# Moving a row of scores through memory in place of TensorE transposes, in a two-layer graph kernel

## The chip, the cores and the metric

The kernel runs on one core of a Trainium2 chip. The metric is device time in microseconds (us) of one execution, lower is better. In the profile of the kernel before, TensorE runs 14264 matrix products and transposes, VectorE and ScalarE run 3909 and 4811 operations, most of them on tiles of 128 partitions, GpSimd does 323 odd jobs, and SyncE is seen only issuing DMAs (transfers). They run side by side (of a span of 2377.1 us TensorE is busy for 2355.3, VectorE for 1988.5), each in the order that the program gives it: with one fetch moved ahead in SyncE's order, a wait of 207.5 us for it goes (e3). For each wait the profile names what ended it. Times are compared with runs of the kernel before taken on the same chip in the same rounds. All repeated runs here were in the normal, fast state; the five single looks (e9 to e11) are of unknown state, so their times are not argued from.

## The reference

128 graphs of 128 tokens with 512 features pass through two layers, all in float32. Layer 0 is multi-head attention weighted by the adjacency matrix. Layer 1 is graph attention:

```python
Wh = jnp.einsum('bsi,io->bso', hidden_state, W)
Wh1 = Wh @ a[:OUT_F, :]
Wh2 = Wh @ a[OUT_F:, :]
e = Wh1 + jnp.swapaxes(Wh2, 1, 2)
e = jax.nn.leaky_relu(e, negative_slope=ALPHA)
attention = jnp.where(adjacent_matrix > 0.5, e, NEG_INF)
attention = jax.nn.softmax(attention, axis=1)
h_prime = jnp.einsum('bst,bto->bso', attention, Wh)
return jax.nn.elu(h_prime)
```

Each token has two scalar scores. The matrix `e` needs one of them along the rows and the other along the columns. In the kernel a token is a partition, so one score is at hand as a number per partition, while the other has to reach all partitions as a row of 128 numbers. How that row gets there is the subject.

## The kernel before

The kernel works on pairs of graphs, 64 in all. A hand-written list (`ORDER`) says in which order the steps of pairs at different stages are issued, for example `pb:2` for "scores of the pair two behind". Each engine keeps to that order. The steps that matter, cut:

```python
def dot1(p, i, k):            # the two scores of each token, on VectorE
    h2, ws = h1s[p]
    ...
        junk, h2[:, i, :], 1.0, (us_sb, ut_sb)[k], ..., accum_out=ws[:, i, k : k + 1]

def scores1(p):               # step "pb": one score to all partitions, on TensorE
    ws = h1s[p][1]
    pb = ps1.tile([P, 2, S], F32, name="pb", tag="ps1")
    for i in range(2):
        nc.tensor.transpose(pb[:, i, :], ws[:, i, 0:1].to_broadcast([P, P]), ident)
    pbs[p] = pb

def mask1(p):                 # step "wm", on VectorE
    wts[p] = work.tile([P, 2, S], F32, name="w", bufs=2)
    nc.vector.scalar_tensor_tensor(wts[p], adjTs.pop(p), 0.5, pbs.pop(p), op0=OP.is_le, op1=OP.subtract)
```

Five transfers matter as well, four of them issued by SyncE. `blocks` and `aT` are a round trip that turns attention weights: 512 KB are written to memory after a transpose on VectorE, and read back in another arrangement. `hA` are the hidden rows of a later pair. `rows` and `mr` are another round trip: GpSimd writes two statistics per token to memory, and SyncE fetches them as one row for all partitions. `hidden` on VectorE then needs `mr`.

```python
def spread0(p):
    ...
    rows0[p] = dram.tile([2, P, 2], F32, name="rows0")
    nc.gpsimd.dma_start(rows0[p].rearrange("b p s -> p b s"), mv)

def fetch0(p):                # step "f0"
    ...
    nc.sync.dma_start(..., r.rearrange("b p s -> (b p s)").partition_broadcast(P))
```

## Time and profile before

| | before |
|---|---|
| median of 4 runs | 2380.38 us |
| span of the profiled run | 2377.1 us |
| TensorE busy / idle | 2355.3 / 21.8 us |
| VectorE busy | 1988.5 us |
| one cycle of two pairs in the middle | 73.08 us |
| granted TensorE clock | 1.000 |

The profile page gives each engine's busy time; "chain that ended last" follows the last instruction back through whatever released it. In its lines PE is TensorE (PEld its weight loads), DVE VectorE, ACT ScalarE, POOL GpSimd and SPq the queue of SyncE; L421 is line 421 of the kernel. The prediction below shows those lines. Two more belong to what follows. They list DMAs with their number, their size and the median time from issue to landing:

```profile
blocks<-tr SPq DMA_DIRECT2D x128, 512.0 KB, 5.1
...
rows<-mv POOLq DMA_DIRECT2D x60, 2.0 KB, 4.6
```

The second is a warning that is easily overlooked: 2 KB take nearly as long (4.6 us) as 512 KB (5.1 us).

### The profile page before, as it was taken

To read this page: it belongs to the slowest core of one execution; us is meant where nothing else is said; L and a number is where in the kernel's file an instruction comes from. 1 tells how busy PE (TensorE), PEld (TensorE's weight loads), DVE (VectorE), ACT (ScalarE), POOL (GpSimd) and SP (SyncE) were. 2 spreads that over 40 slices of the span, in tenths; PEclk is the share of its full clock that TensorE was granted. 3 is DMA by queue.
4 is the path that set the end of the run, shared out by engine and by line. 5 is a ranking of instruction groups with operands and counts; after the bars stand their busy time and mean duration, and the time that the engine had idled before them with its cause. 6 is when DMAs were issued, how large, how long until landed. Compare 5 with 4: busy or idle time off the path is not lost.

```text
span 2377.1 us, 40536 instructions
## 1 busy us (share of the span) xinstructions
PE 2355.3 (99%) x14264; PEld 2062.0 (87%) x14264; DVE 1988.5 (84%) x3909; ACT 1457.4 (61%) x4811; POOL 265.7 (11%) x323
## 2 busy tenths in 40 slices
...
GB/s 173 123 129 116 138 130 121 137 133 129 142 111 126 154 121 138 111 118 158 116 138 133 118 137 137 128 145 107 125 160 116 138 111 123 153 120 125 108 113 93
DMA packets 255275, 306.10 MB, mean 129 GB/s; under 512 B 21856, under 2 KB 181600, under 8 KB 254432
## 3 DMA queue, kind: packets, MB, share of 16 engines
...
HBM read 202.64 MB, written 100.79 MB: 128 GB/s over the span
## 4 chain that ended last, share of the span: by engine, by line
PE 99%; DMA 1%; DVE 0%; ACT 0%; issue 0%; DVEq 0%
PE acc_a L250 28%; PE row_a L291 24%; PE acc_c L250 14%; PE row_c L291 9%; PE acc_b L250 7%; PE sc L312 6%; PE pc L375 5%; PE pg L453 5%; PE pb L421 1%; DMA wk<-in_wkT 0%; PE pm L494 0%; DMA bq<-in_bq 0%; PE pt L189 0%; DVE junk L412 0%; DVE x L479 0%
## 5 line engine op out<-in xcount | busy, mean ns | idle before, releaser
L330 ACT ACTIVATE at<-at,nmx 128x128 f32<-128x128 f32 x1024 | 397.0, 393 | 23.0 <-DVE nmx L325 22.0
L291 PE MATMUL row_a<-w,gT 128*128 128x256 f32 x1280 | 325.4, 385 | 2.8 <-DVE z L471 1.7
L339 ACT ACTIVATE at<-at,rs 128x128 f32<-128x128 f32 x1024 | 317.8, 390 | 15.3 <-DVE rs L334 15.2
L291 PE MATMUL row_a<-wo,cxT 128*128 128x256 f32 x1280 | 319.5, 380 | 0.4 <-DVE cxT L148 0.4
L164 POOL TENSOR_SCALAR mv<-mv 128x2 f32<-128x2 f32 x128 | 78.9, 616 | 2057.8 <-DVE mv L161 1999.3
L467 ACT COPY z<-row_a 128x256 f32<-128x256 f32 x256 | 92.6, 362 | 298.5 <-PE row_a L291 297.9
L291 PEld LDWEIGHTS row_a<-w,gT 128*128 128x128 f32 x1280 | 237.3, 190 | 42.0 <-DVE z L471 2.5
L291 PEld LDWEIGHTS row_a<-wo,cxT 128*128 128x128 f32 x1280 | 233.8, 190 | 28.1 <-DVE cxT L148 0.6
L318 DVE SCALAR_TENSOR_TENSOR at<-sc,adj 128x1024 f32<-128x1024 f32 x128 | 156.7, 1225 | 92.2 <-PE sc L312 89.7
L267 ACT ACTIVATE kT<-acc_a,bk 128x256 f32<-128x256 f32 x256 | 107.3, 470 | 156.7 <-PE acc_a L250 155.1
L330 ACT ACTIVATION_READ_ACCUMULATOR at<-at,nmx 128x1 f32 x1024 | 195.5, 191 | 0.0
L346 DVE STREAM_TRANSPOSE tr<-at 128x1024 f32<-128x1024 f32 x128 | 158.7, 1240 | 33.0 <-ACT at L339 29.8
L160 DVE BATCH_NORM_STATS2 st<-x 128x6 f32<-128x512 f32 x256 | 175.3, 685 | 10.9 <-DMA x<-in_x 6.7
L389 DVE TENSOR_TENSOR x<-row_a,x 128x256 f32<-128x256 f32 x320 | 132.8, 415 | 50.6 <-PE row_a L291 48.3
L262 ACT COPY v<-acc_a 128x512 f32<-128x512 f32 x128 | 74.7, 584 | 150.0 <-PE acc_a L250 150.0
L325 DVE TENSOR_REDUCE nmx<-at 128x8 f32<-128x1024 f32 x128 | 156.1, 1220 | 4.2
L382 ACT COPY cxT<-pc 128x512 f32<-128x512 f32 x128 | 74.9, 585 | 127.3 <-PE pc L375 127.1
L312 PEld LDWEIGHTS sc<-kT,qT 64*128 64x128 f32 x2048 | 124.2, 187 | 32.4 <-issue 32.0
L312 PE MATMUL sc<-kT,qT 64*128 64x128 f32 x2048 | 148.7, 285 | 0.0
L165 POOL TENSOR_TENSOR mv<-mv,mhalf 128x2 f32<-128x2 f32 x128 | 140.2, 1095 | 10.7
L453 PEld LDWEIGHTS pg<-w,h 128*128 128x128 f32 x1024 | 133.7, 192 | 6.6 <-ACT z L467 0.2
L453 PE MATMUL pg<-w,h 128*128 128x128 f32 x1024 | 134.4, 275 | 0.0
...
## 6 DMA issues: line engine op xcount, KB each, us to landing
blocks<-tr SPq DMA_DIRECT2D x128, 512.0 KB, 5.1
aT<-blocks SPq DMA_DIRECT2D x512, 128.0 KB, 3.0
x<-in_x SPq DMA_DIRECT2D x123, 512.0 KB, 5.4
out<-x SPq DMA_DIRECT2D x64, 512.0 KB, 5.5
...
```

The source lines that it names most:

```text
L160: nc.vector.bn_stats(st, src[:, i, :])
L165: nc.gpsimd.tensor_tensor(mv[:, :, 1], mv[:, :, 1], mhalf.to_broadcast([P, 2]), OP.pow)
L250: nc.tensor.matmul(acc[:, m, :], lhsT, rhs, start=fresh and m == 0 and c == 0, stop=c == 1, skip_group_check=True)
L291: nc.tensor.matmul(acc, left[:, la, c, :], w[:, wb, c, :], start=n in (0, 3) and c == 0, stop=c == 1, skip_group_check=True)
L312: nc.tensor.matmul(sc[:, s * C + j, :], qT[r, j, cols], kT[r, j, cols], start=True, stop=True)
L318: nc.vector.scalar_tensor_tensor(at, scs.pop(b), QSCALE, adjs[p][:, i : i + 1, :].to_broadcast([P, H, S]), op0=OP.mult, op1=OP.mult)
L325: nc.vector.tensor_reduce(nmx, at, AX.X, OP.max, negate=True)
L330: nc.scalar.activation(at[:, j, :], at[:, j, :], AF.Exp, bias=nmx[:, j : j + 1], accum_out=sums[:, j : j + 1])
L339: nc.scalar.activation(at[:, j, :], at[:, j, :], AF.Copy, scale=rs[:, j : j + 1])
L346: nc.vector.transpose(trs[b], at.rearrange("p h (j k) -> p j h k", k=Q))
L389: nc.vector.tensor_tensor(d, row_acc(p, "o", bank), d, OP.add)
L453: nc.tensor.matmul(pg[:, c, :], h1s[p][0][:, i, c * P : (c + 1) * P], wts[p][:, i, :], start=True, stop=True)
```

## The change

TensorE is the bound, so take the 128 small transposes away from it, except in the last two pairs, where little other work would hide a round trip. In their place GpSimd writes the scores to memory, and SyncE reads them back into all partitions, straight into the tile that the mask operation then overwrites. The orders for the head, the loop and the tail were chosen anew.

```diff
+    def send_scores1(p):                                  # step "pd"
+        pbs[p] = dram.tile([2, P], F32, name="row1")
+        with nc.allow_non_contiguous_dma(reason="a number of a row"):
+            nc.gpsimd.dma_start(pbs[p].rearrange("b p -> p b"), h1s[p][1][:, :, 0])
+
+    def spread_scores1(p):                                # step "pv"
+        r = pbs[p]
+        pbs[p] = wts[p] = work.tile([P, 2, S], F32, name="w", bufs=2)
+        nc.sync.dma_start(
+            wts[p].rearrange("p b s -> p (b s)"), r.rearrange("b p -> (b p)").partition_broadcast(P)
+        )
 ...
+        if p < N - 2:
+            table.pop("pb")
+            table |= {"pd": lambda: send_scores1(p), "pv": lambda: spread_scores1(p)}
 ... (HEAD, ORDER and TAIL replaced; the part of the new ORDER that matters:)
+    d00:2 peb:1 d01:2 pd:2 ... fla:0 ... bla:0 w1:3 pv:2 ... lT:0 ... pla:0 ... f0:0 ... wm:2
```

On SyncE the new loop order reads: block send (`bla`), spread (`pv`), hidden rows (`lT`), block fetch (`pla`), statistics (`f0`).

More of the change, by code (lines that the diff above doesn't have):

```diff
@@ L422, in scores1 @@
         pbs[p] = pb
+    def send_scores1(p):
[8 more added lines that the diff above has]
+        )
     def mask1(p):
-        wts[p] = work.tile([P, 2, S], F32, name="w", bufs=2)
+        if p not in wts:
+            wts[p] = work.tile([P, 2, S], F32, name="w", bufs=2)
         nc.vector.scalar_tensor_tensor(wts[p], adjTs.pop(p), 0.5, pbs.pop(p), op0=OP.is_le, op1=OP.subtract)
@@ L535 @@
     HEAD = """
-        lx@0 t0@-5 Lu0@0 t1@-5 lt@0 Lq@0 Lk@0 pp@0 lx@1 hn0@0 hn1@0 tp0@0 Wq0@0 Lu1@0 t1@-4 t0@-4 tp1@0 pp@1 Wq2@0 hn0@1
-        ev0@0 Lv@0 ev1@0 U3@-1 U5@-1 Wk0@0 U1@-2 lx@2 hn1@1 F1@-2 tp1@1 Lo@0 tp0@1 Wq1@0 la@-1 Lw@0 ev0@1 la@0 ev1@1
-        t1@-3 t0@-3 U8@-2 U6@-2 F3@-1 pp@2 l0@-2 U2@-2 hs0@-3 F6@-2 l0@-1 hs1@-3 Wk1@0 U10@-2 Wv0@0 Lc@0 Wk2@0 Wk3@0
-        hn0@2 hs2@-3 U7@-1 F7@-1 Wv1@0 A5@-1 hs3@-3 t0@-2 U3@-2 F10@-2 t1@-2 pp@3 A8@-2 hn1@3 tp0@2 U2@-1 U9@-1 hn0@3
-        hn1@2 F3@-2 cu01@0 F2@-1 U4@-1 F9@-1 tp1@2 cu00@0 U8@-1 l0@0 ev0@2 ev1@2 A9@-1 U10@-1 tp0@3 Ww0@0 l0@1 t0@-1
@@ L541 @@
-        U11@-1 U5@-2 F4@-1 t1@-1 F10@-1 sca@0 F5@-2 tp1@3 ata@0 mxa@0 exa2@0 exa3@0 exa0@0 ccp@0 A2@-2 Wv2@0 ccd@0 U1@0
-        ev0@3 t1@0 sh@0 ev1@3 rca1@0 U6@0 U7@-2 nma2@0 Wq3@0 t0@0 F6@0 hs0@-1 cu10@0 s0@-1 nma3@0 exa1@0 U1@-1 rca0@0
-        lt@1 scb@0 hs1@-1 F7@-2 U3@1 nma0@0 nma1@0 A2@-1 fla@0 atb@0 U10@0 mxb@0 U6@-1 exb0@0 Wv3@0 U4@-2 t1@1 bla@0
-        U2@0 exb2@0 A11@-1 exb1@0 rcb0@0 exb3@0 t0@1 nmb0@0 A5@-2 f0@0 rcb1@0 nmb1@0 nmb3@0 pla@0 s0@0 A6@-1 Wo0@0 U9@-2
-        sup0@0 hs2@-1 nmb2@0 sca@1 Wo2@0 f0@1 flb@0 sua0@0 ata@1 blb@0 A9@-2 lT@1 F10@0 U8@0 F3@1 U2@1 A8@0 F1@0 mxa@1
@@ L546 @@
-        plb@0 la@1 cu11@0 hs3@-1 exa2@1 exa0@1 U3@0 F2@1 exa1@1 rca0@1 exa3@1 nma1@1 U5@1 U4@1 U7@1 A2@0 nma0@1 Wo1@0
-        Ww2@0 rca1@1 scb@1 F4@1 Ww1@0 nma3@1 nma2@1 lT@0 F7@1 l0@2 pca@0 F3@0 A5@1 fla@1 pcb@0 pea@0 sup1@0 U9@1 atb@1
-        mxb@1 peb@0 exb2@1 U8@1 U5@0 sua1@0 cs0@0 bla@1 s0@1 Ww3@0 hd0@0 pla@1 hd1@0 exb1@1 o0@0 f0@2 o1@0 F9@1 hd0@1
-        hd1@1 exb3@1 exb0@1 U10@1 od0@0 F10@1 cs1@0 od1@0 rcb1@1 nmb3@1 U1@1 rcb0@1 nmb2@1 F5@0 o2@0 nmb1@1 A9@1 sca@2
-        hs0@1 nmb0@1 A2@1 pca@1 U6@1 od2@0 Wo3@0 cs2@0 o4@0 flb@1 o3@0 ata@2 cs3@0 od4@0 U11@1 od4c@0 blb@1 o5@0 mxa@2
@@ L551 @@
-        o6@0 exa3@2 exa2@2 od5@0 hs2@1 exa0@2 exa1@2 U4@0 t1@2 rca1@2 nma3@2 hs1@1 A5@0 A6@1 od6@0 rca0@2 nma2@2 st0@0
-        U7@0 pea@1 nma0@2 U1@2 A11@1 st1@0 o0@1 plb@1 nma1@2 F7@0 pcb@1 scb@2 sh@1 fla@2 pw@0 peb@1 atb@2 U2@2 o1@1
-        mxb@2 F1@2 bla@2 nm@0 U3@2 h21@0 exb2@2 cs0@1 cs1@1 U4@2 U9@0 h20@0 A2@2 d11@0 od0@1 exb3@2 d00@0 od1@1 hs3@1
-        d10@0 F3@2 o2@1 lT@2 d01@0 od2@1 exb0@2 rcb1@2 pb@0 exb1@2 U5@2 wm@0 rcb0@2 pr@0 F5@2 nmb1@2 cs2@1 U6@2 m1@0
-        o4@1 e1@0 t0@2 lt@2 U7@2 nmb0@2 cs3@1 nmb3@2 A5@2 A9@0 pla@2 sw@0 F7@2 od4@1 o3@1 g0@0 nmb2@2 o5@1 ge0@0 od4c@1
+        lx@0 Lu1@0 Lo@0 Lw@0 t0@-5 lx@1 Lk@0 t1@-5 Lq@0 pp@0 hn0@0 hn1@0 tp0@0 ccp@0 ev0@0 t0@-4 lx@2 Lv@0 t1@-4 Lc@0
@@ new lines @@
+        pp@1 Wk0@0 Lu0@0 Wk2@0 hn0@1 tp1@0 hn1@1 tp0@1 cu10@0 ev1@0 tp1@1 ev0@1 U6@-2 Ww0@0 t0@-3 U3@-1 F6@-2 Ww1@0
+        ev1@1 t1@-3 U5@-1 F3@-1 Wk1@0 l0@-2 pp@2 Wq0@0 la@-1 Wo0@0 U8@-2 Wv0@0 Wq1@0 hs0@-3 U1@-2 hs1@-3 Wk3@0 ccd@0
+        U10@-2 F1@-2 Wv2@0 t0@-2 U7@-1 F10@-2 A5@-1 hn1@2 hn0@2 U2@-1 hs2@-3 F7@-1 t1@-2 Wq2@0 pp@3 U9@-1 F2@-1 hs3@-3
+        A8@-2 hn1@3 tp0@2 F9@-1 Wq3@0 U8@-1 ev0@2 hn0@3 Wv1@0 l0@-1 U4@-1 A9@-1 cu00@0 U10@-1 F4@-1 tp1@2 F10@-1 U3@-2
+        t1@-1 ev1@2 t0@-1 sca@0 F3@-2 l0@0 s0@-1 lt@0 U4@-2 ata@0 mxa@0 tp0@3 tp1@3 ev0@3 cu11@0 U1@0 exa2@0 ev1@3
@@ new lines @@
+        cu01@0 exa3@0 U11@-1 exa1@0 t0@0 exa0@0 f0@0 U5@-2 t1@0 A11@-1 s0@0 rca1@0 rca0@0 hs0@-1 U6@0 F5@-2 hs2@-1
+        nma2@0 sh@1 nma0@0 U2@-2 nma3@0 A5@-2 F1@0 Wv3@0 nma1@0 scb@0 F6@0 fla@0 U1@-1 U9@-2 A2@-1 atb@0 U6@-1 mxb@0
+        A9@-2 exb0@0 U7@-2 Ww3@0 exb1@0 hs1@-1 exb2@0 A6@-1 U3@1 lT@0 rcb0@0 exb3@0 lT@1 nmb0@0 rcb1@0 Wo1@0 U10@0
+        nmb1@0 A2@-2 l0@1 F7@-2 la@0 hs3@-1 nmb2@0 bla@0 sup0@0 nmb3@0 f0@1 sca@1 F3@1 flb@0 F10@0 U3@0 Wo2@0 blb@0 U2@1
+        ata@1 la@1 pla@0 U8@0 F2@1 mxa@1 F3@0 hd0@1 U5@1 exa0@1 plb@0 exa1@1 exa3@1 U7@1 rca0@1 t1@1 nma0@1 sh@0 exa2@1
@@ new lines @@
+        U5@0 nma1@1 A8@0 sua0@0 rca1@1 hd0@0 U4@1 F5@0 t0@1 nma2@1 nma3@1 s0@1 l0@2 scb@1 pca@0 F7@1 pcb@0 pea@0 fla@1
+        U9@1 peb@0 A5@1 bla@1 atb@1 o0@0 F9@1 mxb@1 o1@0 F4@1 exb1@1 U4@0 od0@0 Wo3@0 exb0@1 pla@1 cs0@0 exb3@1 rcb0@1
+        U7@0 cs1@0 hd1@1 nmb0@1 la@2 nmb1@1 od1@0 sup1@0 exb2@1 U10@1 sua1@0 rcb1@1 cs2@0 nmb2@1 hd1@0 U2@0 F10@1 nmb3@1
+        flb@1 o2@0 sca@2 Ww2@0 blb@1 od2@0 o3@0 A2@0 cs3@0 o4@0 A5@0 U9@0 od4@0 ata@2 plb@1 U1@1 od4c@0 mxa@2 o5@0
+        exa2@2 exa1@2 o6@0 od5@0 hs0@1 exa0@2 U1@2 rca0@2 od6@0 nma0@2 st1@0 exa3@2 pca@1 st0@0 scb@2 pea@1 rca1@2 hs1@1
@@ new lines @@
+        pw@0 nma3@2 A2@1 pcb@1 nma1@2 hs2@1 F7@0 U8@1 nma2@2 nm@0 peb@1 fla@2 h20@0 U6@1 h21@0 d00@0 F1@2 A9@1 d10@0
+        o0@1 atb@2 pd@0 U3@2 cs2@1 la@3 cs0@1 mxb@2 o1@1 F3@2 U11@1 cs1@1 exb0@2 od0@1 exb1@2 U5@2 A11@1 od1@1 hs3@1
+        U6@2 A9@0 pv@0 d01@0 bla@2 lT@2 rcb0@2 d11@0 nmb1@2 o2@1 f0@2 F5@2 U4@2 exb2@2 od2@1 exb3@2 F6@2 U7@2 pla@2 A5@2
+        A6@1 rcb1@2 wm@0 nmb2@2 o3@1 cs3@1 F7@2 o4@1 nmb0@2 pr@0 U2@2 od4@1 nmb3@2 od4c@1 m1@0 flb@2 e1@0 o5@1 o6@1
+        blb@2 od5@1 U9@2 od6@1 hd0@2 U10@2 st0@1 st1@1 plb@2 A2@2 pw@1 sw@0 hd1@2
@@ L556 @@
     """
     ORDER = """
-        F4:1 F6:1 flb:1 fb:4 U9:1 F9:1 g1:3 od5:2 ge1:3 o6:2 la:1 st0:2 s0:1 hd0:1 od6:2 U8:1 w0:3 st1:2 gs0:3 blb:1
-        hd1:1 pw:2 w1:3 gs1:3 nm:2 U10:1 zc0:3 so:4 U1:0 gs2:3 h20:2 A9:1 A8:1 l0:0 wd1:3 w2:3 F10:1 gs3:3 h21:2 plb:1
-        lx:1 hs0:1 zc2:3 lT:0 sca:0 pca:1 pcb:1 scb:0 w4:3 d00:2 d01:2 pea:1 A6:1 ata:0 mxa:0 peb:1 d10:2 w3:3 F1:0
-        d11:2 cs0:1 t1:0 exa1:0 f0:0 exa3:0 pb:2 sh:1 A4:4 wm:2 zc4:3 exa2:0 exa0:0 pr:2 o0:1 o1:1 rca1:0 F8:0 nma3:0
@@ L562 @@
-        hs2:1 w5:3 hs1:1 wd4c:3 rca0:0 U2:0 nma1:0 cs2:1 cs1:1 nma2:0 m1:2 nma0:0 w6:3 od0:1 U11:1 od1:1 fla:0 U3:0
-        zc5:3 atb:0 F2:0 mxb:0 F3:0 o2:1 e1:2 A10:16 cs3:1 wd6:3 U5:0 F5:0 sw:2 exb0:0 A2:0 U4:0 exb2:0 A3:28 exb3:0
-        exb1:0 A5:0 A11:1 bla:0 o3:1 rcb1:0 od2:1 nmb2:0 U6:0 hs3:1 o4:1 lt:0 rcb0:0 nmb0:0 t0:0 nmb3:0 nmb1:0 pla:0
-        U7:0 ez:3 F7:0 F11:-22 g0:2 fa:3 od4:1 A1:15 od4c:1 ge0:2 o5:1 A7:14
+        U1:0 F10:1 hs2:1 fb:4 t0:1 g0:3 so:4 g1:3 ge0:3 U2:0 t1:1 ge1:3 lt:2 nm:2 s0:1 F2:0 sca:0 h21:2 h20:2 pca:1
@@ new lines @@
+        ata:0 pcb:1 lx:1 pea:1 mxa:0 l0:0 A7:8 F1:0 scb:0 hs0:1 exa3:0 gs0:3 U4:0 hs1:1 exa2:0 hs3:1 gs2:3 d10:2 exa0:0
+        A2:0 U3:0 exa1:0 rca1:0 d00:2 peb:1 d01:2 pd:2 nma2:0 U8:1 F8:8 nma3:0 cs2:1 cs0:1 F11:-7 rca0:0 A4:8 A3:8 A1:8
+        cs1:1 nma1:0 A9:1 o0:1 nma0:0 gs1:3 o1:1 F4:0 fla:0 F3:0 w0:3 atb:0 bla:0 w1:3 pv:2 U5:0 mxb:0 F5:0 sh:1 zc0:3
+        lT:0 exb3:0 U11:1 od0:1 exb2:0 U6:0 od1:1 A5:0 exb1:0 pla:0 wd1:3 exb0:0 d11:2 o2:1 rcb1:0 A8:1 nmb3:0 U7:0 f0:0
+        od2:1 nmb2:0 A11:1 rcb0:0 cs3:1 nmb1:0 gs3:3 w2:3 wm:2 nmb0:0 F7:0 o4:1 F6:0 o3:1 zc2:3 od4:1 pr:2 flb:0 w3:3
@@ L566 @@
+        U9:0 od4c:1 blb:0 m1:2 F9:0 hd0:0 w4:3 A6:0 o5:1 zc4:3 e1:2 wd4c:3 o6:1 od5:1 plb:0 st0:1 A10:3 w5:3 sw:2 w6:3
+        od6:1 zc5:3 st1:1 la:-1 U10:0 wd6:3 pw:1 hd1:0 ez:3 fa:3
     """
     TAIL = """
-        F4@-5 U9@-5 F9@-5 g1@-7 flb@-5 o6@-6 A6@-5 U10@-5 fb@-8 la@-5 ge1@-7 gs0@-7 F10@-5 so@-8 hd0@-5 od5@-6 blb@-5
-        pca@-5 sca@-4 hd1@-5 pea@-5 la@-4 U5@-3 st0@-6 lx@-5 U8@-5 ata@-4 mxa@-4 exa0@-4 exa3@-4 exa1@-4 od6@-6 w0@-7
-        hs0@-5 w1@-7 o0@-5 scb@-4 exa2@-4 st1@-6 pw@-6 U3@-3 gs2@-7 A9@-5 zc0@-7 nm@-6 rca0@-4 rca1@-4 hs1@-5 wd1@-7
@@ L571 @@
-        nma3@-4 nma0@-4 gs1@-7 nma2@-4 o1@-5 gs3@-7 plb@-5 sh@-5 nma1@-4 fla@-4 pcb@-5 atb@-4 U11@-5 od0@-5 U6@-4 F3@-3
-        h21@-6 peb@-5 h20@-6 mxb@-4 exb0@-4 w2@-7 d10@-6 cs0@-5 exb3@-4 exb2@-4 zc2@-7 U7@-3 cs1@-5 A11@-5 d00@-6
-        exb1@-4 od1@-5 w4@-7 F6@-4 d11@-6 o2@-5 pb@-6 rcb0@-4 od2@-5 rcb1@-4 wm@-6 nmb1@-4 d01@-6 nmb0@-4 sca@-3 w3@-7
-        nmb2@-4 U10@-4 nmb3@-4 zc4@-7 w5@-7 cs2@-5 bla@-4 scb@-3 pr@-6 flb@-4 ata@-3 cs3@-5 hs2@-5 zc5@-7 pla@-4 m1@-6
-        wd4c@-7 pca@-4 mxa@-3 w6@-7 F7@-3 o4@-5 od4@-5 wd6@-7 F10@-4 e1@-6 U2@-3 blb@-4 exa1@-3 exa0@-3 sw@-6 plb@-4
@@ L576 @@
-        fa@-7 exa2@-3 o5@-5 ez@-7 pea@-4 rca0@-3 g1@-6 nma0@-3 exa3@-3 o3@-5 la@-3 od5@-5 U9@-3 st0@-5 rca1@-3 od4c@-5
-        g0@-6 o6@-5 ge1@-6 fb@-7 gs0@-6 o0@-4 A5@-3 nma2@-3 nma3@-3 pcb@-4 ge0@-6 nma1@-3 gs1@-6 w0@-6 o1@-4 fla@-3
-        atb@-3 so@-7 lx@-4 mxb@-3 F9@-3 od6@-5 w1@-6 F2@-3 peb@-4 hs3@-5 cs0@-4 zc0@-6 wd1@-6 st1@-5 U8@-4 U10@-3 pw@-5
-        bla@-3 exb3@-3 exb2@-3 exb1@-3 w2@-6 gs2@-6 gs3@-6 pla@-3 nm@-5 cs1@-4 exb0@-3 cs2@-4 rcb1@-3 la@-2 h21@-5
-        rcb0@-3 zc2@-6 nmb3@-3 A8@-4 U8@-3 nmb2@-3 sh@-4 nmb0@-3 nmb1@-3 F10@-3 w4@-6 od0@-4 d11@-5 cs3@-4 od1@-4 zc4@-6
@@ L581 @@
-        d10@-5 U4@-3 F4@-3 U1@-3 sca@-2 flb@-3 w3@-6 h20@-5 ata@-2 o3@-4 mxa@-2 w5@-6 wd4c@-6 zc5@-6 d00@-5 exa0@-2
-        o2@-4 od2@-4 w6@-6 o4@-4 A2@-3 d01@-5 wd6@-6 exa3@-2 od4@-4 lt@-4 exa1@-2 fa@-6 exa2@-2 pca@-3 ez@-6 U6@-3 pb@-5
-        fb@-6 rca0@-2 blb@-3 o5@-4 od4c@-4 wm@-5 nma0@-2 rca1@-2 pr@-5 od5@-4 nma3@-2 A6@-3 o6@-4 plb@-3 nma1@-2 U1@-4
-        U2@-4 nma2@-2 pcb@-3 m1@-5 scb@-2 st0@-4 pea@-3 od6@-4 st1@-4 fla@-2 e1@-5 A9@-3 so@-6 sw@-5 peb@-3 o0@-3 g1@-5
-        g0@-5 U11@-3 ge1@-5 pw@-4 atb@-2 lx@-3 o1@-3 F1@-4 ge0@-5 cs0@-3 nm@-4 mxb@-2 cs2@-3 h21@-4 exb1@-2 gs0@-5 o3@-3
@@ L586 @@
-        w0@-5 sh@-3 lt@-3 w1@-5 exb0@-2 exb3@-2 h20@-4 gs1@-5 od0@-3 A11@-3 U3@-4 exb2@-2 A2@-4 rcb0@-2 d10@-4 cs1@-3
-        zc0@-5 nmb0@-2 od1@-3 d00@-4 rcb1@-2 cs3@-3 o2@-3 d01@-4 wd1@-5 nmb1@-2 od2@-3 nmb2@-2 nmb3@-2 gs2@-5 sca@-1
-        pb@-4 gs3@-5 w2@-5 o4@-3 zc2@-5 w3@-5 flb@-2 od4@-3 ata@-1 d11@-4 wm@-4 w4@-5 zc4@-5 F3@-4 od4c@-3 o5@-3 pr@-4
-        w5@-5 zc5@-5 U5@-4 wd4c@-5 m1@-4 w6@-5 e1@-4 F5@-4 mxa@-1 o6@-3 od5@-3 st0@-3 sw@-4 exa2@-1 U4@-4 exa1@-1 od6@-3
-        exa0@-1 bla@-2 st1@-3 exa3@-1 g0@-4 pw@-3 g1@-4 wd6@-5 A5@-4 fa@-5 ez@-5 U9@-4 ge1@-4 nm@-3 rca0@-1 h21@-3 fb@-5
@@ L591 @@
-        blb@-2 h20@-3 ge0@-4 U7@-4 w0@-4 rca1@-1 gs0@-4 w1@-4 nma1@-1 nma2@-1 d10@-3 F7@-4 pla@-2 d00@-3 A9@-4 zc0@-4
-        gs1@-4 pb@-3 plb@-2 pca@-2 gs2@-4 d01@-3 d11@-3 nma3@-1 scb@-1 wm@-3 pcb@-2 wd1@-4 nma0@-1 peb@-2 w2@-4 so@-5
-        w3@-4 pr@-3 fla@-1 zc2@-4 w4@-4 atb@-1 lx@-2 pea@-2 mxb@-1 cs0@-2 exb2@-1 m1@-3 gs3@-4 zc4@-4 o0@-2 cs2@-2
-        wd4c@-4 cs1@-2 e1@-3 exb3@-1 o1@-2 sh@-2 exb1@-1 sw@-3 rcb1@-1 od0@-2 w6@-4 bla@-1 exb0@-1 w5@-4 zc5@-4 g1@-3
-        wd6@-4 od1@-2 ez@-4 rcb0@-1 nmb0@-1 o2@-2 nmb3@-1 pla@-1 fa@-4 lt@-2 fb@-4 o3@-2 nmb1@-1 g0@-3 nmb2@-1 ge0@-3
@@ L596 @@
-        ge1@-3 od2@-2 o4@-2 cs3@-2 w0@-3 flb@-1 od4@-2 gs0@-3 gs1@-3 o5@-2 od4c@-2 gs2@-3 o6@-2 so@-4 pca@-1 blb@-1
-        w1@-3 w3@-3 lx@-1 od5@-2 pea@-1 st0@-2 o0@-1 od6@-2 zc0@-3 o1@-1 st1@-2 gs3@-3 pw@-2 wd1@-3 nm@-2 h21@-2 w2@-3
-        sh@-1 od0@-1 od1@-1 h20@-2 zc2@-3 d10@-2 plb@-1 pcb@-1 peb@-1 d01@-2 w4@-3 d00@-2 cs0@-1 pb@-2 cs1@-1 wm@-2
-        d11@-2 o2@-1 zc4@-3 pr@-2 od2@-1 cs2@-1 m1@-2 w5@-3 cs3@-1 o4@-1 od4@-1 zc5@-3 o3@-1 o5@-1 wd4c@-3 e1@-2 od4c@-1
-        sw@-2 o6@-1 w6@-3 od5@-1 st0@-1 g0@-2 od6@-1 st1@-1 g1@-2 lt@-1 wd6@-3 ge0@-2 w0@-2 fa@-3 pw@-1 ge1@-2 gs2@-2
@@ L601 @@
-        w1@-2 ez@-3 nm@-1 gs0@-2 gs1@-2 h21@-1 zc0@-2 d10@-1 wd1@-2 h20@-1 d00@-1 d11@-1 d01@-1 w2@-2 pb@-1 zc2@-2 wm@-1
-        pr@-1 gs3@-2 w4@-2 zc4@-2 m1@-1 w3@-2 wd4c@-2 e1@-1 sw@-1 w5@-2 w6@-2 g0@-1 wd6@-2 g1@-1 zc5@-2 ge0@-1 ge1@-1
-        fb@-3 fa@-2 w0@-1 w1@-1 ez@-2 gs0@-1 gs2@-1 zc0@-1 gs1@-1 w3@-1 gs3@-1 wd1@-1 w2@-1 zc2@-1 w4@-1 fb@-2 zc4@-1
-        wd4c@-1 w5@-1 so@-3 so@-2 w6@-1 zc5@-1 wd6@-1 ez@-1 fa@-1 fb@-1 so@-1
+        g1@-7 g0@-7 ge1@-7 hs2@-5 F10@-5 U3@-3 fb@-8 nm@-6 so@-8 h21@-6 sca@-4 ge0@-7 pca@-5 ata@-4 pcb@-5 mxa@-4 scb@-4
@@ new lines @@
+        lx@-5 hs0@-5 exa3@-4 lt@-6 U8@-5 gs0@-7 exa2@-4 gs1@-7 h20@-6 U6@-4 exa1@-4 A9@-5 rca1@-4 exa0@-4 hs1@-5 d10@-6
+        nma2@-4 w0@-7 F6@-4 rca0@-4 d01@-6 U11@-5 pea@-5 d00@-6 nma0@-4 hs3@-5 pd@-6 nma3@-4 w1@-7 nma1@-4 peb@-5 U10@-4
+        fla@-4 zc0@-7 gs2@-7 wd1@-7 o0@-5 F10@-4 atb@-4 o1@-5 mxb@-4 w3@-7 pv@-6 bla@-4 U2@-3 A11@-5 exb1@-4 sh@-5
+        exb2@-4 w2@-7 exb0@-4 cs0@-5 cs1@-5 od0@-5 U8@-4 zc2@-7 od1@-5 exb3@-4 gs3@-7 rcb0@-4 pla@-4 rcb1@-4 w4@-7 A8@-4
+        d11@-6 o2@-5 zc4@-7 nmb3@-4 w5@-7 nmb2@-4 od2@-5 cs2@-5 nmb1@-4 sca@-3 wm@-6 wd4c@-7 nmb0@-4 cs3@-5 pr@-6 o4@-5
@@ new lines @@
+        flb@-4 zc5@-7 F3@-3 o3@-5 od4@-5 blb@-4 F2@-3 ata@-3 w6@-7 la@-3 U4@-3 mxa@-3 wd6@-7 m1@-6 o5@-5 ez@-7 fa@-7
+        plb@-4 U7@-3 exa3@-3 fb@-7 e1@-6 exa2@-3 U5@-3 lt@-5 sw@-6 od4c@-5 so@-7 exa0@-3 rca1@-3 od5@-5 st0@-5 exa1@-3
+        g0@-6 nma3@-3 g1@-6 o6@-5 ge1@-6 nma2@-3 scb@-3 lx@-4 od6@-5 rca0@-3 st1@-5 nma1@-3 pca@-4 nma0@-3 pw@-5 F7@-3
+        pcb@-4 fla@-3 F4@-3 U9@-3 pea@-4 atb@-3 bla@-3 ge0@-6 peb@-4 mxb@-3 w0@-6 F9@-3 o0@-4 gs0@-6 exb0@-3 gs1@-6
+        nm@-5 cs0@-4 w1@-6 h20@-5 U8@-3 d00@-5 zc0@-6 h21@-5 A5@-3 exb1@-3 d10@-5 o1@-4 exb2@-3 wd1@-6 pd@-5 sh@-4
```

28 lines of the change are left out of this document (27 added, 1 removed).

## The prediction

> **What bounds the kernel now.** I read the page from the top: busy shares, then the slices, then the chain that ended last, then the stretches, and last the groups of matmuls.
>
> ```profile
> PE 2355.3 (99%) x14264; PEld 2062.0 (87%) x14264; DVE 1988.5 (84%) x3909; ACT 1457.4 (61%) x4811; POOL 265.7 (11%) x323
> ...
> PE 99%; DMA 1%; DVE 0%; ACT 0%; issue 0%; DVEq 0%
> ```
>
> TensorE is busy for 2355.3 of 2377.1 us, and the chain followed back from the last instruction is TensorE for 99% of the span. A busy share alone would not prove a bound, so the next thing to look at is a stretch in the middle that is one full cycle of the loop (two pairs, 73.08 us: score matmuls start 37.44 and 35.64 us apart in turn).
>
> ```profile
> 1000.00:1073.08 73.08, 73.08 (x446) 64.19 (x445) 61.82 (x121) 45.34 (x151) 8.68 (x10) 1.00 0.48 128
> ```
>
> The columns are the length of the stretch, then the busy time of TensorE, its weight loads, VectorE, ScalarE and GpSimd, then the clock, the DMA share and GB/s. TensorE has no gap at all, VectorE has 11.3 us to spare and DMA is half used. So in the middle the time is simply the sum of the TensorE issue intervals, and only taking work from TensorE shortens it. The 21.8 us in which TensorE is idle lie at the two ends: 7.26 us until the first transpose, 3.94 us waiting for weights, some 7.2 us after the last matmul (2369.9), and under 4 us in short waits of the last pairs.
>
> Now what the changed operation costs. The group line and the chain of waits, in order of time, around one instance:
>
> ```profile
> L421 PE MATMUL pb<-ident,ws 128*128 128x128 f32 x128 | 24.5, 273 | 0.2 <-DVE junk L412 0.2
> ```
>
> ```profile
> 1205.67 0.86 PE row_c L291 x4
> 1206.54 0.22 PE pb L421 x2
> 1206.75 2.59 PE row_a L291 x12
> ```
>
> The group line says 24.5 us and 273 ns each, but 273 ns is the time one matmul takes from start to end, and its tail lies beside the next one. The chain shows what it takes out of the stream: the two transposes of a pair hold TensorE for 0.22 us (1206.54 to 1206.75), and the matmul before keeps its usual 0.86 us for four. This is the number to use, not 24.5 us.
>
> [...] the first eight weight products show 3.53 us, later eights 1.89 us. [...] a 2 KB write of row statistics lands in 4.8 us in the middle, as long as a 512 KB block write (5.2 us), so it is latency that it costs and not bandwidth. [...] 414 ns for the mask operation, which reads PSUM, against 425 ns for the normalising product of the same 128x256 size, which reads SBUF. I count it as unchanged.
>
> **The change part by part.**
> First, removed from TensorE: the two transposes in 62 of 64 pairs. Taking start to next start in the timeline of TensorE for the first 62 pairs, they sum to 13.8 us (0.22 us nearly everywhere, up to 0.32 in three of them). With every other matmul kept and TensorE the bound, this comes off one for one: -13.8 us.
>
> Second, added: per pair a GpSimd DMA of 256 single numbers to memory, and a SyncE DMA of 1 KB to each of 128 partitions (128 KB). 62 of the latter are 8.1 MB on 306 MB, at a DMA share of 0.48: hidden. GpSimd needs some 0.76 us per issue (the row of the existing statistics write) and is 88% idle. What matters is latency. From the order of the changed kernel on VectorE, between the dot products that the send needs and the block transpose that the SyncE queue awaits just before the spread, there are about 4.5 us of VectorE work. The existing write of this sort takes 4.8 us to land, so the queue may wait some 0.5 to 1 us there. Between that block transpose and the mask operation lie about 9 us of VectorE work (1.22 + 1.22 + 1.2 for the three large ones, 0.84 for two additions, and nine small ones of 0.17 to 0.77 us). The existing 256 KB broadcast lands 5.1 us after issue, so about 0.4 + 1 + 5.1 = 6.5 us stand against 9: hidden with some 2.5 us to spare. Cost: 0.
>
> Third, the scores tile leaves PSUM, one of six rotating buffers for about 1 us per pair: TensorE waits for none now, so gain 0. The w tile is taken earlier, but it has two buffers and its former user, two pairs back, is gathered before that: 0.
>
> Fourth, the orders. In the middle TensorE can't be better than gap-free, so a new order there can only lose. Scores and contexts still stand as one block of four per pair, so the slow row switches beside them (about 0.1 us before and 0.1 after) stay. At the start the weights come in another order: now wo and w1 are fetched before wk and wq. Before, the first weight product starts when wk has landed:
>
> ```profile
> 7.26 1.97 PE L189 MATMUL pt<-ident,hn 128*128 128x128 f32 x8 [7.26 <-DVE hn L182]
> 13.16 3.53 PE L250 MATMUL acc_a<-hA,wk 128*128 128x256 f32 x8 [3.94 <-DMA wk<-in_wkT]
> 16.53 1.89 PE L250 MATMUL acc_b<-hA,wk 128*128 128x256 f32 x8
> ```
>
> After, about 5.5 MB must land before the first wq product. In the trace of before, 4.85 MB had landed by 17.5 us (wv) and DMA then moves over 0.4 MB per us, so wq lands at some 18 to 19.5 us, 5 to 6 us later than now. But 4.5 us of work are drawn into the gap: the 16 matmuls of the constant product (3.45 us) and eight more transposes of hidden rows (1.04 us)[...]. Net: -6.2 + 5.5, about -0.5 us, give or take 2. Behind it VectorE has some 10 us of weight sums and hidden sums to do before the first product with such a sum, and TensorE 8.6 us of products: a stall of 0 to 1.5 us there. Start: 0 give or take 2.5. The last two pairs keep the transposes and end with the same steps: 0 give or take 1.5.
>
> Sum: 2380.5 - 13.8 + 0 = 2366.7. As whoever searched the orders anew searched for a shorter run, I lean the ends by -1.5: about 2365 us, 0.65% less.
>
> **The rivals.**
> The round trip shows: the mask operation waits for the broadcast, VectorE runs in order and stops, and TensorE stops behind it. For: VectorE is 85% busy, so a stop of over 1.7 us per pair could no longer be made up; two DMA latencies in series. Against: 9 us of other work, and a SyncE queue that already waits long without harm. If it showed by 0.3 us per pair it would cost 18 us and leave about 2384.
>
> The transposes cost their 24.5 us of the group line, not 13.8: then 2380.5 - 24 = about 2356. For: a switch between kinds of matmul can delay neighbours. Against: the neighbours in the chain keep their 0.86 us.
>
> The ends decide: a worse start (wq late, then VectorE behind) costs up to 5 us, a better one gains as much: 2360 to 2371. For: the start is wholly rearranged. Against: TensorE work moved into the gap balances it.
>
> The new DMAs delay others: block writes wait behind the broadcast, contexts come late. Against: half of the DMA time is free. It would show as waits of the context matmuls, with perhaps 5 us.
>
> **Range and chances.** Steady gain 13.8 give or take 1; ends give or take 4; a small chance of a partial wait. Predicted 2365 us, 8 in 10 between 2358 and 2372. Two per cent is 47.6 us: TensorE would have to lose more than three times all the transposes' time for faster (1%), and only a serious stall in every pair makes it slower (1%). Within 2%: 98%.
>
> **What would show it right or wrong.** Right: TensorE busy falls by about 14 us, to some 2341, still 99% of the span; a cycle of two pairs shrinks from 73.08 to about 72.65 us and stays gap-free; the mask operation has next to no wait for a DMA and still takes about 415 ns; only four transposes of scores remain; the first weight product starts near 18 us with the constant product ahead of it. Wrong: a row in which the mask operation waits for the w tile's DMA, gaps of TensorE in the middle, a cycle longer than 72.9 us, or TensorE idle at the start or end changed by more than 4 us.

## The result, and the profile after

| | before | after |
|---|---|---|
| median | 2380.38 us | 2513.14 us |
| lowest to highest | 2379.18 to 2381.16 | 2509.58 to 2525.98 |
| ratio of the fast runs (95% interval) | | 1.0572 (1.0538 to 1.0605) |

The kernel got 5.6% to 5.7% slower. A ratio is the mean time of one kernel's fast runs over that of the other's of the same rounds, so not quite the ratio of the medians.

The page of the profiled run (span 2524.1 us), its engine line and its chain:

```profile
PE 2385.9 (95%) x14140; PEld 2070.5 (82%) x14140; DVE 1979.8 (78%) x3909; ACT 1464.3 (58%) x4811; POOL 267.4 (11%) x385
...
PE 42%; DMA 29%; DVE 17%; ACT 6%; SPq 4%; issue 3%; ACTq 0%; DVEq 0%
```

The chain is the quickest diagnosis. Before it was TensorE for 99%; now TensorE is 42% of it and DMA 29%. TensorE has 124 instructions less to run, yet it is busy 30.6 us longer (2385.9 against 2355.3), and idle for 138.2 us in place of 21.8. The sum of the two rises, 30.6 + 116.4 = 147.0 us, is the whole difference of the spans. Part of the longer busy time lies just behind the longer gaps. The granted clock of this run was 0.987, and after 3.82 us of idling twelve matmuls took 4.4 us (1097.42 to 1101.80), with a granted clock of 0.61 in that stretch:

```profile
1097.42 1.95 PE L291 MATMUL row_c<-w,gT 128*128 128x256 f32 x4 [3.82 <-DVE z L485]
1099.16 2.81 PE L250 MATMUL acc_a<-hA,wk 128*128 128x256 f32 x8
```

After a gap of 1.80 us, as many took 2.7 us (1057.91 to 1060.61), at a granted clock of 1.00. Of the 57 stops of this kind (before `row_c`) in the trace, 16 of the 26 that lasted over 2.04 us have such a slow stretch behind them (granted clock 0.50 to 0.66 in the 4.4 us that follow), and none of the 31 others has (1.00). So in this run a gap could cost twice, once as a gap and once as slower matmuls behind it.

Who waits for whom (total us, times, longest us), first the engines, then SyncE's queue:

```profile
DVE hA L214 <- DMA mr<-rows: 207.5, 53, 5.5
PEld row_c L291 <- DVE z L485: 132.2, 57, 4.9
PE row_c L291 <- DVE z L485: 109.3, 57, 4.5
DVE w L441 <- DMA w<-row: 125.2, 61, 5.4
```

```profile
SPq L433 <- DMA row<-ws: 305.5, 62, 16.7
```

VectorE waits for two DMAs in nearly every pair: for the spread scores (`w<-row`, the new one) and for the row statistics (`mr`, an old one that the change did not touch). TensorE's own wait, before `row_c`, is for a VectorE addition (`z`) that merely stands behind those waits in VectorE's order. And SyncE stands still for 305.5 us at the spread, waiting until the send has landed.

The DMAs, median us to landing in the last column:

```profile
blocks<-tr SPq DMA_DIRECT2D x128, 512.0 KB, 6.9
...
hA<-in_xT SPq DMA_DIRECT2D x120, 256.0 KB, 7.3
mr<-rows SPq DMA_DIRECT2D x60, 256.0 KB, 6.9
...
w<-row SPq DMA_DIRECT2D x62, 128.0 KB, 5.5
row<-ws POOLq DMA_DIRECT2D x62, 1.0 KB, 8.6
```

The send of 1 KB is the slowest of all, at 8.6 us. One pair of it in the timeline (start us, us, engine, what; in brackets the idle time before and what ended it):

```profile
1035.20 0.72 POOL L428 DMA_DIRECT2D row<-ws  x1 [5.40 <-DVE junk L412]
...
1039.08 0.34 SPq L350 DMA_DIRECT2D blocks<-tr  x1
...
1043.87 0.34 SPq L433 DMA_DIRECT2D w<-row  x1
...
1044.34 3.37 SPq L90 DMA_DIRECT2D hA<-in_xT  x2
...
1047.75 2.23 SPq L356 DMA_DIRECT2D aT<-blocks  x4
...
1049.77 0.42 DVE L441 SCALAR_TENSOR_TENSOR w<-adjT,w 128x256 f32<-128x256 f32 x1 [2.22 <-DMA w<-row]
...
1050.03 0.43 SPq L205 DMA_DIRECT2D mr<-rows  x1
...
1056.30 1.22 DVE L214 TENSOR_TENSOR hA<-hA,mr 128x1024 f32<-128x1024 f32 x1 [3.99 <-DMA mr<-rows]
...
1057.91 1.13 PE L291 MATMUL row_c<-w,gT 128*128 128x256 f32 x4 [1.80 <-DVE z L485]
```

The send goes out at 1035.20. SyncE has sent its blocks by 1039.4 and then stands until 1043.87, when the send has landed. Only then do the spread, the hidden rows, the block fetch and the statistics leave, in that order. VectorE waits 2.22 us for the first and 3.99 us for the last, and TensorE stops for 1.80 us.

### The profile page after: what moved, and what is told of

Read it like the earlier page. It is cut to its first block, busy times and chain, and to the rows that moved or that the text cites. A ratio compares the mean times of both kernels' runs of the same rounds, so it can differ in the third digit from the quotient of the medians.

```text
span 2524.1 us, 40974 instructions
## 1 busy us (share of the span) xinstructions
PE 2385.9 (95%) x14140; PEld 2070.5 (82%) x14140; DVE 1979.8 (78%) x3909; ACT 1464.3 (58%) x4811; POOL 267.4 (11%) x385
## 4 chain that ended last, share of the span: by engine, by line
PE 42%; DMA 29%; DVE 17%; ACT 6%; SPq 4%; issue 3%; ACTq 0%; DVEq 0%
PE acc_a L250 14%; DMA mr<-rows 14%; DMA blocks<-tr 11%; PE acc_c L250 5%; PE pg L467 4%; PE row_a L291 4%; PE acc_b L250 4%; PE sc L312 4%; PE row_c L291 4%; SPq L356 3%; DVE hA L214 3%; ACT at L339 3%; ACT at L330 3%; DVE at L318 2%; DVE nmx L325 2%
## 5 line engine op out<-in xcount | busy, mean ns | idle before, releaser
L291 PE MATMUL row_a<-w,gT 128*128 128x256 f32 x1280 | 320.2, 380 | 3.6 <-DVE z L485 2.0
L291 PEld LDWEIGHTS row_a<-wo,cxT 128*128 128x128 f32 x1280 | 243.5, 190 | 34.2 <-DVE x L389 0.9
L214 DVE TENSOR_TENSOR hA<-hA,mr 128x1024 f32<-128x1024 f32 x60 | 73.5, 1225 | 230.2 <-DMA mr<-rows 207.5
L291 PE MATMUL row_c<-w,gT 128*128 128x256 f32 x512 | 147.9, 414 | 109.3 <-DVE z L485 109.3
L490 ACT ACTIVATE ez<-z 128x1024 f32<-128x1024 f32 x64 | 67.8, 1059 | 284.3 <-DVE z L485 284.3
L164 POOL TENSOR_SCALAR mv<-mv 128x2 f32<-128x2 f32 x128 | 29.1, 227 | 1874.5 <-DVE mv L161 1622.8
L291 PEld LDWEIGHTS row_c<-w,gT 128*128 128x128 f32 x512 | 97.3, 199 | 144.2 <-DVE z L485 132.2
L389 DVE TENSOR_TENSOR x<-row_a,x 128x256 f32<-128x256 f32 x320 | 134.5, 420 | 27.5 <-PE row_a L291 18.8
L165 POOL TENSOR_TENSOR mv<-mv,mhalf 128x2 f32<-128x2 f32 x128 | 146.6, 1145 | 10.7
```

The costliest lines, as they stand in the source:

```text
L165: nc.gpsimd.tensor_tensor(mv[:, :, 1], mv[:, :, 1], mhalf.to_broadcast([P, 2]), OP.pow)
L214: nc.vector.tensor_tensor(h, h, row, OP.subtract)
L291: nc.tensor.matmul(acc, left[:, la, c, :], w[:, wb, c, :], start=n in (0, 3) and c == 0, stop=c == 1, skip_group_check=True)
L389: nc.vector.tensor_tensor(d, row_acc(p, "o", bank), d, OP.add)
```

## The experiments

There were three things to tell apart: the new orders, the waiting for the send, and what the send does to other transfers. Thirteen kernels were run. Most are the changed kernel with one edit. A first form of e1, with the transposes at the spread's place, could not be built; that attempt left nothing in the record, so its cause is not shown. In e1 the transposes therefore stand beside the mask operation.

### e1: the new orders with the old transposes

```diff
-            table |= {"pd": lambda: send_scores1(p), "pv": lambda: spread_scores1(p)}
+            table["wm"] = lambda: (scores1(p), mask1(p))
```

> The changed kernel's orders, but every pair's scores by TensorE transposes again (issued with the mask operation), no send and no spread. Theory A (the two DMAs of the scores are what slows the changed kernel): about 2380 us, 2370 to 2395, and a gap-free cycle. Rival B (the orders chosen anew are bad by themselves, e.g. the row statistics are fetched too late): over 2450 us, with VectorE still waiting for the fetched row statistics.

Measured: 2379.43 us, ratio 1.0001 (0.9993 to 1.0010). The new orders are neither better nor worse; a cycle takes 73.0 us, gap-free. Rival B falls: the slowdown is wholly in the two DMAs. This run is also the clean reference for landing times in the new orders:

```profile
blocks<-tr SPq DMA_DIRECT2D x128, 512.0 KB, 2.7
```

2.7 us, where the changed kernel has 6.9.

### e2: the spread doesn't wait for the send

```diff
-            ..., r.rearrange("b p -> (b p)").partition_broadcast(P)
+            ..., bass.AP(tensor=a1.tensor, offset=a1.offset, ap=[[0, P], [1, 2 * S]])
```

The send is still made, but the spread reads an input; results are wrong on purpose.

> The send stays, but the spread reads the same 1 KB of an input, so it waits for no send (results wrong on purpose). Theory A1 (SyncE's queue stands still at the spread until the send has landed, and the hidden-row loads, block fetches and row statistics behind it are late): most of the loss goes, 2360 to 2390 us, the wait of VectorE for the row statistics falls from 207 us to under 40. Rival A2 (the second hop or the added DMA traffic is what costs): stays above 2450 us.

Measured: 2453.98 us, ratio 1.0318 (1.0286 to 1.0349). Theory A1 missed its number. Rival A2 met its own, though by only 4 us, with one run of four (2446.57) below the limit; e5 to e8 show which part of the added traffic it is. Taking the wait away gives back 59 us (2513.1 to 2454.0), and 90 us more than the later e5 remain. The statistics wait fell only to 154.5 us, and that of the mask operation to 90.6. The DMA list says why:

```profile
blocks<-tr SPq DMA_DIRECT2D x128, 512.0 KB, 7.0
...
w<-in_a SPq DMA_DIRECT2D x62, 128.0 KB, 9.0
row<-ws POOLq DMA_DIRECT2D x62, 1.0 KB, 11.3
```

Nothing waits for the send now, and yet the block writes and even the spread, both issued while it is under way, land late. SyncE's queue shows how that reaches the statistics: the block fetch stands ahead of them and has to wait for the block write.

```profile
SPq L356 <- DMA blocks<-tr: 565.0, 124, 9.4
```

In e1 this wait is 200.8 us. So with the wait at the spread gone, the queue stands at the block fetch instead. That was a new theory (C below): the send slows other transfers.

### e3: the statistics fetched ahead of the blocks and the spread

```diff
-    ... bla:0 w1:3 pv:2 ... U7:0 f0:0 od2:1
+    ... f0:0 bla:0 w1:3 pv:2 ... U7:0 od2:1
```

> In the loop the fetch of the row statistics stands ahead of the block send and the spread on SyncE's queue, all else as changed. Theory A1 with the late statistics as the main loss (VectorE waits 207 us for them, 125 us for the scores): 2400 to 2450 us, the statistics wait near zero, the scores wait stays at 100 us or more. If the scores' own wait at the mask operation is what counts: 2480 us or more.

Measured: 2437.78 us, ratio 1.0246 (1.0216 to 1.0275), as expected. The wait for the statistics is gone from the list, while the mask operation now waits 211.4 us for the spread. So the place in SyncE's queue is worth 75 us (2513.1 to 2437.8), but cannot mend it: SyncE now waits 392.6 us for the send.

### e4: the send issued by SyncE

```diff
-            nc.gpsimd.dma_start(pbs[p].rearrange("b p -> p b"), h1s[p][1][:, :, 0])
+            nc.sync.dma_start(pbs[p].rearrange("b p -> p b"), h1s[p][1][:, :, 0])
```

> The send is issued by SyncE in place of GpSimd. If GpSimd's way of sending is what makes it land after a median of 7.4 us, it lands in 2 to 4 us and the time is 2365 to 2400 us. If 256 single numbers are slow from any queue: landing 6 us or more and 2480 us or more.

Measured: 2597.38 us, ratio 1.0914 (1.0897 to 1.0930), the slowest of all. The send lands in 9.1 us from this queue too, so it is not GpSimd's way of sending that is slow. (The 7.4 us of the expectation were a median over sends and spreads together; the sends alone had 8.6.) And SyncE now also waits for the dot products ahead of it (307.7 us).

### e5: the spread without any send

```diff
     def send_scores1(p):
-        pbs[p] = dram.tile([2, P], F32, name="row1")
-        ...
+        pbs[p] = None
```

The spread reads an input as in e2; wrong results on purpose.

> No send at all; the spread reads the same 1 KB of an input (results wrong on purpose). Theory C (the send of 256 single numbers slows every other transfer while it is under way: block writes landed in 2.7 us without it and in 7.0 us with it, even where nothing waited for it): 2358 to 2375 us, block writes landing in about 3 us, no wait of VectorE for the spread. Rival D (the spread itself, 128 readers of one KB, is what crowds the queues): stays above 2420 us and block writes at 6 us or more.

Measured: 2363.59 us, ratio 0.9939 (0.9924 to 0.9954). Block writes land in 2.9 us, the spread in 4.2 us, and the mask operation no longer appears in the list of waits.

```profile
blocks<-tr SPq DMA_DIRECT2D x128, 512.0 KB, 2.9
```

So the spread, with its 8 MB, is hidden entirely, and without the send the loss is gone. Against e2 the only difference is the send, which nobody awaits there: 90 us.

### e6: the send alone, which nobody reads

```diff
+            table |= {"pd": lambda: send_scores1(p), "wm": lambda: (scores1(p), mask1(p))}
```

(in place of both steps; scores by transposes)

> Scores by transposes as in e1 and, beside them, the send of 256 single numbers to memory that nobody reads. Theory C: block writes land in 6 to 8 us against 2.7 us in e1, and the time is 2395 to 2460 us though nothing waits for the send. Rival D: 2380 us, as e1, with block writes at about 3 us.

Measured: 2382.32 us, ratio 1.0014 (1.0007 to 1.0021). Theory C has the direction right and missed both its numbers. The block writes do land late (5.6 us, just under its range) and so do the hidden rows (6.0 us against 3.8 in e1), though not the fetch of the statistics (3.5 against 4.1), which leaves later. But the time rises by only 3 us over e1, where I expected 15 or more. The slow-down of other transfers is real, and here the loop makes up for nearly all of it. VectorE waits for the statistics for 27.0 us in all.

```profile
blocks<-tr SPq DMA_DIRECT2D x128, 512.0 KB, 5.6
...
hA<-in_xT SPq DMA_DIRECT2D x120, 256.0 KB, 6.0
...
row<-ws POOLq DMA_DIRECT2D x62, 1.0 KB, 8.9
```

### e7: the same send, with the numbers 512 B apart

```diff
-        pbs[p] = dram.tile([2, P], F32, name="row1")
-            nc.gpsimd.dma_start(pbs[p].rearrange("b p -> p b"), h1s[p][1][:, :, 0])
+        far = dram.tile([P, 2, P], F32, name="row1")
+            nc.gpsimd.dma_start(far[:, :, 0], h1s[p][1][:, :, 0])
```

> As e6, but every number is written 512 B from the next in place of 4 B. Theory C1 (the small writes hinder each other because they fall into the same stretch of memory): the send lands in 2 to 4 us, block writes in about 3 us, time about 2380 us. Theory C2 (each single number costs as such, wherever it goes): as e6.

Measured: 2379.85 us, ratio 1.0004 (0.9996 to 1.0013), and

```profile
blocks<-tr SPq DMA_DIRECT2D x128, 512.0 KB, 2.6
...
hA<-in_xT SPq DMA_DIRECT2D x120, 256.0 KB, 3.6
...
row<-ws POOLq DMA_DIRECT2D x62, 1.0 KB, 2.0
```

The same 256 numbers of 4 B, from the same queue at the same place, land in 2.0 us in place of 8.9, and the transfers behind them are as quick as without any send. So here it is not the number of small writes that costs but that they lie side by side.

### e8: fewer and longer runs

The kernel already uses VectorE's transpose for `blocks`. The scores are kept in columns of a 32-wide tile, turned with it in blocks of 32x32, and then lie as four runs of 32 numbers per graph (e8, which reads them back so, gives correct results):

```diff
-        with nc.allow_non_contiguous_dma(reason="a number of a row"):
-            nc.gpsimd.dma_start(pbs[p].rearrange("b p -> p b"), h1s[p][1][:, :, 0])
+        wts[p] = work.tile([P, 2, S], F32, name="w", bufs=2)
+        wt = wts[p][:, 0, 0:Q]
+        nc.vector.transpose(wt, h1s[p][1])
+        for i in range(2):
+            nc.gpsimd.dma_start(pbs[p][i].rearrange("(j k) -> j k", k=Q), wt[i :: Q, :])
```

(with `h1s[p][1]` now one of two zeroed tiles `[P, Q]`, Q = 32, whose column `2 * k + i` takes score k of graph i; the turned scores borrow the tile that the spread overwrites)

> The changed kernel, but VectorE turns the scores in blocks of 32x32 first (about 0.1 to 0.2 us per pair, of 11 us that it has spare in two pairs), so the send is 8 runs of 128 B and not 256 numbers of 4 B. Theory C: the send lands in 2 to 4 us, block writes in about 3 us, 2358 to 2375 us, faster than both kernels. If the round trip costs by itself: above 2420 us.

Measured: 2363.72 us, ratio 0.9939 (0.9923 to 0.9956), correct, and faster than both kernels: 0.6% against the kernel before, under the 2% that the verdict asks for but with an interval clear of 1. The engine line, the chain, a stretch of about one cycle, and the DMAs:

```profile
PE 2340.3 (99%) x14140; PEld 2054.8 (87%) x14140; DVE 1996.7 (85%) x3971; ACT 1459.9 (62%) x4811; POOL 292.8 (12%) x449
...
PE 98%; ACT 1%; DMA 0%; DVE 0%; issue 0%; ACTq 0%; DVEq 0%
```

```profile
1000.00:1072.60 72.60, 72.60 (x442) 64.00 (x441) 61.97 (x124) 45.47 (x151) 9.36 (x14) 1.00 0.49 135
```

```profile
blocks<-tr SPq DMA_DIRECT2D x128, 512.0 KB, 2.8
...
w<-row SPq DMA_DIRECT2D x62, 128.0 KB, 4.1
row<-w POOLq DMA_DIRECT2D x124, 0.5 KB, 1.6
```

This is the kernel that the prediction described: TensorE gap-free in the middle, a cycle of 72.57 us (from a `pg` group of matmuls at 1005.90 us to the next but one at 1078.47), and sends that land in 1.6 us. SyncE waits for it 33.5 us in all, against 305.5. GpSimd, which keeps to its order too, waits 427.1 us for the turned scores ahead of its sends, more than the 322.2 us for which it waits in the changed kernel, so its standing there is not what slowed that one. The turning costs 62 instructions of 211 ns on VectorE, 13.1 us, which VectorE has to spare.

### e9 to e11: how close is too close

Single looks at e7 with another distance, `dram.tile([P, 2, n])` with n = 1, 4, 16 and 2, and at e6 with half of the numbers.

> As e7 (transposes, and a send that nobody reads), the two numbers of a token side by side and the tokens 8 B apart, so 256 numbers 4 B apart in 1 KB. If crowding alone counts: the send lands in about 9 us, as in e6 (8.9). If e7 was fast because of the order of its dimensions: about 2 us.

> As e7, numbers 16 B apart. If the time over 2.0 us (e7) goes with the number of writes that fall into one stretch of memory (6.9 us at 4 B in e6): 2.0 + 6.9/4 = about 3.7 us to landing. If anything closer than 512 B is slow: about 9 us.

> As e7, numbers 64 B apart. Same rule: 2.0 + 6.9/16 = about 2.4 us. If anything closer than 512 B is slow: about 9 us.

> As e6, but only the 128 numbers of the first graph of a pair, still 4 B apart. If the writes wait for each other within a stretch of 512 B (two such stretches in e6, side by side): 8.9 us as e6. If all writes of the send wait for each other: 2.0 + 6.9/2 = about 5.5 us.

> As e7, numbers 8 B apart. The landing was 8.4 us at 4 B and 2.0 us at 16 B, and the existing write of the row statistics (pairs of 8 B side by side) lands in 5.5 us. If closeness in bytes alone sets it: between 3 and 6 us. If there is a step just above 4 B: about 2 us; if the step is just under 16 B: 8 us or more.

e10's edit:

```diff
-            nc.gpsimd.dma_start(pbs[p].rearrange("b p -> p b"), h1s[p][1][:, :, 0])
+            nc.gpsimd.dma_start(pbs[p].rearrange("b p -> p b")[:, 0:1], h1s[p][1][:, 0:1, 0])
```

| run | numbers, distance | send lands (median us) | block writes land | time (us) |
|---|---|---|---|---|
| e6 | 256, 4 B (graph by graph) | 8.9 | 5.6 | 2382.32 |
| e9_apart_4B | 256, 4 B (token by token) | 8.4 | 5.0 | 2385.78 |
| e10 | 128, 4 B | 8.5 | 4.5 | 2380.48 |
| e11 | 256, 8 B | 3.9 | 2.9 | 2380.50 |
| e9_apart_16B | 256, 16 B | 2.0 | 2.6 | 2380.15 |
| e9_apart_64B | 256, 64 B | 2.0 | 2.6 | 2378.44 |
| e7 | 256, 512 B | 2.0 | 2.6 | 2379.85 |

The order of the dimensions doesn't matter (e9_apart_4B). My proportional rule was wrong: it gave 3.7 us for 16 B and 2.4 us for 64 B, and both land in 2.0. The landing time about halves with each doubling of the distance from 4 to 16 B and then stands at a floor. The number of writes doesn't set it either: half as many at 4 B take just as long (e10). (That count is the program's; the trace books 32 packets for every send, in e6, e7 and e10 alike.) That fits the first of the two guesses on record for e10, writes that wait for each other within a stretch of memory while different stretches go on side by side. As a mechanism it stays a guess: what in the memory or in the DMA engines does this, no run here shows. The times of the single looks are one run each and decide nothing; the landing times are medians of 62 sends in one execution.

## Why the prediction was wrong

The predicted 2365 us was missed by 148 us, and a slowdown of over 2% had been given 1%. By its own steps:

**The bound, and the part removed: right.** TensorE was the bound and the transposes' worth was their 0.22 us in the stream. Where the rest doesn't interfere, in e5 and e8, the kernel takes 2363.6 and 2363.7 us, with TensorE busy 2339.9 and 2340.3 us (predicted 2341) and a cycle of 72.57 us (predicted 72.65). The rival that counted 24.5 us falls: e8 is 15.0 us faster than the kernel before in its rounds (2378.74). That this lies so near to 2365 is in part luck: TensorE idles 21.8 us in e8, as it did before, so the 1.5 us leaned off the ends were not there, while its busy time fell by 15.0 us and not 13.8. What the other 1.2 us are is not shown. The delay of neighbours that this rival appealed to is in the trace of the kernel before, but elsewhere: beside the score matmuls, four `row_a` matmuls take 0.96 us from start to next start just before them (1199.50 to 1200.46) and 0.97 us just after (1204.54 to 1205.51), in place of 0.86.

**"The orders": right.** e1 shows them neutral (2379.43 against 2379.27 us in the same rounds). The 6.2 us that the prediction takes off at the start are 4.5 us of work drawn into the gap and the 1.7 us that it counted for slower matmuls after the gap: the first eight weight products took 3.53 us, later eights 1.89 us. The trace gives a granted clock of 1.00 for that stretch (13.16 to 16.53), so why they were slower is not shown. The start came as described; in the changed kernel's timeline of TensorE:

```profile
11.34 5.79 PE L508 MATMUL pm<-wo,bv 128*128 128x256 f32 x16 [2.62 <-DMA bv<-in_bv]
16.96 1.60 PE L189 MATMUL pt<-ident,hn 128*128 128x128 f32 x12
18.40 1.89 PE L250 MATMUL acc_a<-hA,wq 128*128 128x256 f32 x8
```

The constant product fills the gap at a slower pace than counted (5.79 us in place of 3.45), after a wait for `bv` that the prediction lacks. The weights `wq` landed at 18.0 us (predicted 18 to 19.5), and the first weight product starts at 18.40. The stall behind it did not come.

**The spread, "hidden": right as to the spread itself.** In e5 it lands in 4.2 us and nothing waits.

**The mask operation "unchanged": right.** It takes 425 ns from SBUF in the changed kernel and 415 in e8, against 414 from PSUM.

**The failed step** is this: "The existing write of this sort takes 4.8 us to land, so the queue may wait some 0.5 to 1 us there", and with it the sum "0.4 + 1 + 5.1 = 6.5 us stand against 9". I took the landing time of another write, one with the same number of pieces, and treated it as pure latency that depends neither on the shape of the destination nor on anything else. It was a write of 8 B pieces in a row, and pieces of 4 B in a row took 8.6 us. (It may be slow for the same reason; no run spaced it.) In the pair shown above the other terms hold: the send left 3.9 us before the block write (1035.20 to 1039.08; 4.5 predicted), and VectorE had about 8.5 us of work from its transpose to the wait (1039.05 to 1047.55; 9 predicted). But SyncE stood for 4.8 us, and 5.9 us passed from the issue of the spread to the mask operation: 10.7 us against 8.5, and VectorE waited for the 2.2 us between. Two more things follow from the slow send, and neither was in the sum:

- SyncE waited 305.5 us at the spread, some 5 us per pair in place of 0.5 to 1. I checked what the spread itself would make late, and not what stood behind it in SyncE's queue. The statistics stood there: VectorE waited 207.5 us for them, more than for the scores. Taking only the wait away gave back 59 us (e2).
- The slow send held up other transfers, with block writes landing in 6.9 us in place of 2.7. Taking the send away too gave back another 90 us (e2 to e5). The split into 59 and 90 depends on the order of removal: the slow send by itself, with the transposes kept, costs only 3 us (e6). The rival "The new DMAs delay others" had the right transfers but blamed the broadcast, which e5 clears, and I held against it that "half of the DMA time is free". That mean share (0.48) didn't show a 1 KB transfer that takes 9 us to land.

The rival "the round trip shows" named the chain that came (mask operation, then VectorE, then TensorE), with a limit of 1.7 us per pair that its own lines don't give (11.3 us to spare in two pairs are 5.6 us per pair). The measured waits of VectorE are 125.2 + 207.5 us over 62 pairs, about 5.4 us per pair, and a good part was made up: the loss against e5 is 149.5 us, 2.4 us per pair. Its size was misjudged because its input, the landing time, was.

What stays open: why the send's interference costs 3 us in e6 and 90 us in e2. At the block fetch SyncE waits 392.6 us in e6 and 565.0 us in e2. The queue's reserve, its wait for VectorE ahead of a block write (`SPq L350 <- DVE x L389`), is 314.4 us in e1, 130.9 in e6 and only 48.4 in e2. In e2 the mask operation also waits for the late spread (90.6 us), which uses up VectorE's slack before the late statistics come. That is an argument from the waits, and no run separates the two.
